# 128 bytes left free ahead of layer 0's weight tiles in a two-layer graph network

## The chip, the cores and the metric

The kernel runs on one core of one Trainium2 chip. The metric is the device time of one execution in microseconds (us); three runs of the kernel before took 1934.32, 1938.56 and 1939.16, so the median is 1938.56. A profiled execution has a span of 1935.9 us.

On-chip memory (SBUF) has 128 partitions. A tile has the same address, counted in bytes from the start of the partition, in all of them, and this document calls that number its address.

## What is computed

There are 4096 nodes with 512 features and a dense 4096x4096 adjacency matrix `adj` that is mostly zeros. The reference, cut to what matters:

```python
# layer 0
bw = sign(L0_gnn_weight); ba = max(sign(x), 0)
xw = ba @ bw.T
x = layernorm(x + relu(adj @ xw))
# layer 1
node_att = softmax(x @ node_w, axis=0)
h = x @ edge_w
e = where(adj > 0, h @ h.T, NEG_BIG)
edge_att = softmax(e, axis=1)
output = (adj * node_att * edge_att) @ (x @ weight) + bias
x = layernorm(x + output)
```

Layer 0 holds one small product (`ba @ bw.T`) and one large one (`adj @ xw`, 4096x4096 by 4096x512). Layer 1 holds the attention scores `h @ h.T` (4096x4096) and a second product of that size by 4096x512.

## The kernel before

Everything is cut into blocks of P = 128 rows: NB = 32 blocks of nodes, KD = 4 blocks of features, W = 512 columns for the moving operand of a matmul. A matmul on TensorE (PE) has two operands in SBUF: the stationary one, 128x128, which a weight load (LDWEIGHTS, "PEld" in the profile) brings into the array, and the moving one, here 512 columns wide, which streams through it. In `nc.tensor.matmul(out, a, b)`, `a` is the stationary and `b` the moving operand.

**Layer 0, first part.** `whole(g)` makes 512 rows of `xw` at a time, for g = 0 to 7. DVE turns a piece of x into 0/1 signs (`ba`, lines 186, 187, 211, 212) and the weights into signs (`bw`, lines 204 and 206); the matmuls of line 214 have `ba` as the stationary and `bw` as the moving operand; the results go to the large tile `xw` (lines 220 to 223). Two sign values are packed into one number, which is why a matmul of line 214 serves two blocks of rows. Before the first data land, line 200 runs matmuls on the tile `warm`, which holds zeros; further ones fill gaps between the first matmuls of line 214.

**Layer 0, second part.** For each block of 128 rows of `adj` (loop over `n`), the block arrives in two loads of 1 MB (`at`, line 358). Each half is handled in two quarters of 8 blocks of 128 columns. ACT casts a quarter to fp32r (`hi`, line 363), DVE subtracts to get what the cast lost (`lo`, line 365), and PE multiplies both by the same rows of `xw`:

```python
for c in range(QC):
    kb = half * HB + q * QC + c
    nc.tensor.matmul(acc, hi[:, c, :], xw[:, kb, :], start=(kb == 0), stop=False)
    nc.tensor.matmul(acc, lo[:, c, :], xw[:, kb, :], start=False, stop=(kb == NB - 1))
```

These are lines 373 and 374: 64 matmuls for each of 30 blocks, all 128x128 by 128x512 in fp32r. The other two blocks (`early`) are multiplied by `follow(g)` (lines 246 and 247) between the steps of the first part, in the same way. `hi` and `lo` have two buffers each. After a block is done, `rest` normalises it on DVE and ACT, PE transposes it (line 333), and pieces go to HBM for layer 1. Beside this, `premask` loads pieces of `adj` on the ACT queue and writes masks.

**Layer 1.** Line 101 makes `h`, lines 641 and 714 the scores, line 1081 the second large product; line 603 transposes. All of these matmuls are in fp32, and their operands are `hT`, `lops`, `right`, `slot`, `lent` and `lop`.

**What sets the order.** The tile framework orders instructions by its own costs and dependencies, except on DVE and ACT in the main loop of layer 0, where the written order holds (`manual_schedule`). Each engine works through its own list and waits for semaphores.

**Where tiles lie.** Pools are laid out one after the other in the order in which they are opened: `const`, `big`, `rows`, `small`, then for layer 0 `wide`, `stream`, `weights` (`wp`), `signs` (`sp`). Inside a pool, tiles with different tags follow each other. `big` holds one tile of 64 KB, called here the large buffer: it is `xw` in layer 0, later `hT`, then `over`. `wp` begins with `warm`, followed by `bw`, `us`, `ba` and smaller tiles; tiles with the same tag share a place (`bw`, `pair` and `we_s`; `us` and `ends`; `ba`, `single` and `sums_l`). `sp` holds the two buffers of `lo` and then those of `hi`. The pools of layer 1 (`slots`, `lopp`, `pan`) are opened after those of layer 0 are closed and take their space again from the end of `small`.

Addresses of the tiles that PE reads in layer 0, in the kernel before:

| tile | role in a matmul | address | remainder by 512 |
|---|---|---|---|
| xw | moving, lines 246, 247, 373, 374 | 17472 | 64 |
| bw | moving, line 214 | 182848 | 64 |
| ba | stationary, line 214 | 195136 and 199232 | 64 |
| lo | stationary, lines 247, 374 | 209472 and 213568 | 64 |
| hi | stationary, lines 246, 373 | 217664 and 221760 | 64 |

One row block of `xw` is 2048 bytes long, one block of `hi`, `lo` or `ba` 512.

Of the kernel before, what the change touches and what calls it, by code (L numbers as in the profile page):

```python
# [11 lines left out]
F32 = mybir.dt.float32  # L12
# [6 lines left out]
P = 128  # L19
# [10 lines left out]
def kernel(  # L30
# [13 lines left out]
    nc = tc.nc  # L44
# [114 lines left out]
    with (  # L159
# [5 lines left out]
        x1T = wide.tile([P, KD, N], F32, name="x1T")  # L165

        warm = wp.tile([P, W], BF16, name="warm")
        nc.vector.memset(warm, 0.0)
        w0 = stream.tile([P, KD, D], F32, name="w0", tag="stream")

# [1286 lines left out]
```

## Time and profile before

| what | value |
|---|---|
| median of three runs | 1938.56 us |
| span of the profiled execution | 1935.9 us |
| PE busy | 1916.8 us (99%) |
| weight loads busy | 1203.3 us (62%) |
| DVE busy | 1390.0 us (72%) |
| ACT busy | 1022.9 us (53%) |
| GpSimd (POOL) busy | 291.9 us (15%) |
| matmuls | 6742 |
| DMA traffic | 508.72 MB, mean 263 GB/s |
| first and last matmul of lines 373 and 374 start at | 57.3 us, 507.0 us |

Busy time of PE is from the start of a matmul to its modelled end, and successive matmuls overlap, so neither the busy share nor the mean duration of a matmul tells how many fit into a stretch of time. For that one reads the distance between the starts of successive matmuls, here called the spacing. A group line gives the source line, the engine, the operation, the tiles (result<-operands), the shape and the count, then the busy time in us and the mean duration in ns, then the idle time of that engine just before these instructions and what ended it.

### The profile page before, as it was taken

To read this page: it belongs to the slowest core of one execution; us is meant where nothing else is said; L and a number is where in the kernel's file an instruction comes from. 1 tells how busy PE (TensorE), PEld (TensorE's weight loads), DVE (VectorE), ACT (ScalarE), POOL (GpSimd) and SP (SyncE) were. 2 spreads that over 40 slices of the span, in tenths; PEclk is the share of its full clock that TensorE was granted. 3 is DMA by queue.
4 is the path that set the end of the run, shared out by engine and by line. 5 is a ranking of instruction groups with operands and counts; after the bars stand their busy time and mean duration, and the time that the engine had idled before them with its cause. 6 is when DMAs were issued, how large, how long until landed. Compare 5 with 4: busy or idle time off the path is not lost.

```text
span 1935.9 us, 20238 instructions
## 1 busy us (share of the span) xinstructions
PE 1916.8 (99%) x6742; PEld 1203.3 (62%) x6742; DVE 1390.0 (72%) x2062; ACT 1022.9 (53%) x1614; POOL 291.9 (15%) x413
## 2 busy tenths in 40 slices
PE   9999999999999999999999999999999999999998
PEld 6888888888644445454555444456666666666655
DVE  7766676676765567566664996687869987798737
ACT  5433333333202567576677675546766577757731
POOL 0122222222341101011111111111111110111100
PEclk9999999999999999999999999999999999999999
DMA  8888888888475478577783998777778777877731
GB/s 309 295 326 308 298 315 313 322 310 292 153 268 219 156 259 313 188 275 254 290 309 104 346 342 288 259 273 257 269 263 293 260 269 262 294 274 258 272 110 44
DMA packets 169527, 508.72 MB, mean 263 GB/s; under 512 B 15696, under 2 KB 41040, under 8 KB 161744
## 3 DMA queue, kind: packets, MB, share of 16 engines
q1 hardware_dynamic: 89472, 226.39, 35.0%
q0 software_dynamic: 64688, 239.10, 32.9%
q10 hardware_dynamic: 15264, 41.95, 5.9%
q8 instruction: 53, 0.87, 0.2%
q14 instruction: 50, 0.41, 0.1%
HBM read 385.74 MB, written 121.63 MB: 262 GB/s over the span
## 4 chain that ended last, share of the span: by engine, by line
PE 81%; DVE 9%; issue 4%; DMA 4%; ACT 1%; POOL 0%; POOLq 0%; DVEq 0%; SPq 0%
PE bank L1081 26%; PE seven L714 14%; PE acc L374 11%; PE acc L373 11%; PE pe L641 6%; PE seven L101 4%; PE po L1208 3%; PE pt L603 2%; DMA slot<-s_d 1%; DVE lent L847 1%; DMA lent<-s_d 1%; PE acc L246 1%; PE pw L214 1%; DVE lent L835 1%; PE pt L333 1%
## 5 line engine op out<-in xcount | busy, mean ns | idle before, releaser
L1081 PE MATMUL bank<-lent,lop 128*128 128x512 f32 (+1 forms) x1136 | 420.0, 517 | 0.0
L373 PE MATMUL acc<-xw,hi 128*128 128x512 f32 x960 | 376.4, 392 | 0.0
L374 PE MATMUL acc<-xw,lo 128*128 128x512 f32 x960 | 374.3, 390 | 0.0
L1081 PE MATMUL bank<-slot,lop 128*128 128x256 f32 (+1 forms) x1052 | 356.1, 486 | 1.6 <-DVE slot L862 1.6
L1081 PEld LDWEIGHTS bank<-lent,lop 128*128 128x128 f32 x1136 | 215.7, 190 | 173.9 <-issue 159.3
L1081 PEld LDWEIGHTS bank<-slot,lop 128*128 128x128 f32 x1052 | 199.6, 190 | 135.3 <-issue 115.8
L363 ACT CAST hi<-at 128x1024 fp32r<-128x1024 f32 x120 | 126.4, 1054 | 203.4 <-PE acc L373 148.4
L365 DVE TENSOR_TENSOR lo<-at,hi 128x1024 fp32r<-128x1024 f32 x120 | 147.0, 1225 | 85.2 <-ACT hi L363 85.2
L374 PEld LDWEIGHTS acc<-xw,lo 128*128 128x128 f32 x960 | 180.3, 188 | 37.1 <-DVE lo L365 0.3
L373 PEld LDWEIGHTS acc<-xw,hi 128*128 128x128 f32 x960 | 180.3, 188 | 36.7
L1090 ACT COPY over<-bank 128x512 f32<-128x512 f32 x200 | 114.4, 581 | 111.6 <-PE bank L1081 99.4
L641 PE MATMUL pe<-hT 128*128 128x512 f32 (+3 forms) x384 | 132.1, 486 | 0.0
L574 ACT ACTIVATE line<-line,nmax_c 128x512 f32<-128x512 f32 x160 | 114.8, 724 | 22.5 <-DVE nmax_c L565 22.3
L565 DVE CUSTOM_DVE_ANT_0 line<-lent,slot 128x512 f32<-128x512 bf16 x140 | 90.7, 689 | 48.4 <-ACT slot L651 26.6
L835 DVE CUSTOM_DVE_ANT_1 lent<-lent,line 128x2048 f32<-128x2048 f32 x40 | 91.4, 2286 | 20.8 <-DMA lent<-s_d 12.0
L838 ACT ACTIVATE lent<-lent 128x2048 f32<-128x2048 f32 x40 | 76.5, 1912 | 53.1 <-DVE lent L835 53.0
L841 ACT ACTIVATE slot<-slot 128x2048 f32<-128x2048 f32 x36 | 68.8, 1912 | 65.2 <-DMA slot<-in_adj_t_dram 58.3
L641 PEld LDWEIGHTS pe<-hT 128*128 128x128 f32 x384 | 64.6, 191 | 41.4 <-issue 33.8
L714 PE MATMUL seven<-hT 128*128 128x512 f32 x192 | 89.8, 593 | 0.0
L1053 ACT COPY bank<-over 128x512 f32<-128x512 f32 x144 | 84.9, 595 | 3.0 <-DVE left L973 0.2
L603 PEld LDWEIGHTS pt<-ident,lent 128*128 128x128 f32 x418 | 52.2, 141 | 52.1 <-issue 38.8
L604 ACT COPY slot<-pt 128x512 f32<-128x512 f32 (+3 forms) x123 | 68.5, 559 | 23.9 <-PE pt L603 23.9
(262 smaller groups left out, 2850.3 us busy)
## 6 DMA issues: line engine op xcount, KB each, us to landing
at<-in_adj_t_dram SPq DMA_DIRECT2D x60, 1024.0 KB, 6.8
lop<-lop_d SPq DMA_DIRECT2D x79, 512.0 KB, 4.7
lent<-s_d POOLq DMA_DIRECT2D x39, 1024.0 KB, 7.4
slot<-in_adj_t_dram POOLq DMA_DIRECT2D x38, 1024.0 KB, 7.0
s_d<-slot POOLq DMA_DIRECT2D x30, 1024.0 KB, 7.1
lent<-in_adj_t_dram POOLq DMA_DIRECT2D x26, 1024.0 KB, 7.4
lop<-lop_d SPq DMA_DIRECT2D x99, 256.0 KB, 4.2
lent<-in_adj_dram SPq DMA_DIRECT2D x48, 512.0 KB, 5.3
```

The costliest lines, as they stand in the source:

```text
L363: nc.scalar.copy(hi, aq)
L365: nc.vector.tensor_sub(lo, aq, hi.bitcast(F32))
L373: nc.tensor.matmul(acc, hi[:, c, :], xw[:, kb, :], start=(kb == 0), stop=False)
L374: nc.tensor.matmul(acc, lo[:, c, :], xw[:, kb, :], start=False, stop=(kb == NB - 1))
L565: nc.vector.tensor_tensor_reduce(line, mask, src, -1.0, HUGE, ALU.add, ALU.min, accum_out=nmax_c[:, b, c : c + 1])
L574: nc.scalar.activation(line, line, AF.Exp, bias=nmax_c[:, b, c : c + 1], scale=-1.0, accum_out=sum_c[:, b, c : c + 1])
L603: nc.tensor.transpose(pt[:, j, :], src[:, ts(j, P)], ident)
L641: nc.tensor.matmul(pe[:, lo * P :], hT[:, k, ts(A * BG + i, P)], hT[:, k, (B * BG + lo) * P : (B + 1) * W], start=(k == 0), stop=(k == KD ...
L714: nc.tensor.matmul(ps, left[m][:, k, q, :], right[m][:, k, :], start=(first and k == 0), stop=(k == KD // 2 - 1), skip_group_check=not first,)
L835: pinned[0](nc.vector._custom_dve(TENSOR_ADD_SAT, out=q, in0=q, in1=m, s0=0.0, s1=-HUGE))
L1081: nc.tensor.matmul(ps, lop[:, k, :], rop[:, k, :], start=start, stop=(k == K - 1), skip_group_check=True)
L1090: nc.scalar.copy(self.to(), self.bank[:, : self.w])
```

## The change

A tile of 32 fp32 numbers per partition, 128 bytes, is opened in the pool `wp` right behind `warm`, and set to zero once so that it is a written tile. Nothing reads it. All that follows in `wp`, and the pool `sp` behind it, has addresses higher by 128: `bw` 182976, `ba` 195264 and 199360, `lo` 209600 and 213696, `hi` 217792 and 221888. The large buffer with `xw` stays at 17472, and so do the tiles of layer 1. It is for changing where the two operands of layer 0's matmuls lie towards each other, with the same work.

```diff
         x1T = wide.tile([P, KD, N], F32, name="x1T")
 
         warm = wp.tile([P, W], BF16, name="warm")
+        room_w = wp.tile([P, 32], F32, name="room_w")
+        nc.vector.memset(room_w, 0.0)
         nc.vector.memset(warm, 0.0)
         w0 = stream.tile([P, KD, D], F32, name="w0", tag="stream")
```

Line numbers in this document are those of the kernel before; behind the added lines they are higher by two in the kernel after.

## The prediction

> **What bounds the kernel now.** The page's first two parts come first: who is busy, and at what clock.
>
> ```profile
> PE 1916.8 (99%) x6742; PEld 1203.3 (62%) x6742; DVE 1390.0 (72%) x2062; ACT 1022.9 (53%) x1614; POOL 291.9 (15%) x413
> ...
> PEclk9999999999999999999999999999999999999999
> ```
>
> PE is busy 99% of the span at full clock, so time moves only if a matmul's spacing changes or PE is made to wait. Next, the chain that ended last, by line:
>
> ```profile
> PE bank L1081 26%; PE seven L714 14%; PE acc L374 11%; PE acc L373 11%; PE pe L641 6%; PE seven L101 4%; PE po L1208 3%; PE pt L603 2%; DMA slot<-s_d 1%; DVE lent L847 1%; DMA lent<-s_d 1%; PE acc L246 1%; PE pw L214 1%; DVE lent L835 1%; PE pt L333 1%
> ```
>
> Tiles that the change moves are read by PE in L373 and L374 (22% together), L246, L247 and L214, and all of these belong to layer 0; the 26% of L1081 and 14% of L714 read other tiles, which stay. The stage by its window (columns: stretch and length; busy time of PE, weight load, DVE, ACT, POOL; clock; DMA share; GB/s):
>
> ```profile
> 48.00:512.00 464.00, 463.99 (x2094) 381.42 (x2093) 323.98 (x497) 154.72 (x193) 108.01 (x151) 1.00 0.83 301
> ```
>
> PE has no gap in 464 us, while DVE has 140 us free, ACT 309 us, and the DMA engines 17%. The groups of that stage say who waits for whom:
>
> ```profile
> L373 PE MATMUL acc<-xw,hi 128*128 128x512 f32 x960 | 376.4, 392 | 0.0
> L374 PE MATMUL acc<-xw,lo 128*128 128x512 f32 x960 | 374.3, 390 | 0.0
> ...
> L363 ACT CAST hi<-at 128x1024 fp32r<-128x1024 f32 x120 | 126.4, 1054 | 203.4 <-PE acc L373 148.4
> L365 DVE TENSOR_TENSOR lo<-at,hi 128x1024 fp32r<-128x1024 f32 x120 | 147.0, 1225 | 85.2 <-ACT hi L363 85.2
> ```
>
> ACT waits 148 us for PE to free a hi buffer; PE waits for neither. The 392 ns are one matmul from start to modelled end and overlap with the next, so the price is the spacing of starts, read from the timeline (start, duration, engine):
>
> ```profile
> 300.09 0.39 PE L374 MATMUL acc<-xw,lo 128*128 128x512 f32 x1
> 300.09 0.19 PEld L373 LDWEIGHTS acc<-xw,hi 128*128 128x128 f32 x1
> 300.32 0.39 PE L373 MATMUL acc<-xw,hi 128*128 128x512 f32 x1
> 300.32 0.19 PEld L374 LDWEIGHTS acc<-xw,lo 128*128 128x128 f32 x1
> ...
> 301.45 0.39 PE L374 MATMUL acc<-xw,lo 128*128 128x512 f32 x1
> ```
>
> From 300.09 to 301.45 are six steps: 0.227 us each. Each weight load starts with the matmul before it and takes 0.19 us, inside 0.227, so the length of the load is not what spaces the matmuls. Other matmuls of this trace are spaced closer for the same 512 columns:
>
> ```profile
> 1124.72 4.03 PE L1081 MATMUL bank<-lent,lop 128*128 128x512 f32 x9
> ```
>
> ```profile
> 10.00 1.04 PE L200 MATMUL idle<-warm 128*128 128x512 bf16 x4
> ```
>
> Nine fp32 matmuls take (4.03 - 0.59)/8 = 0.430 us each, twice 0.215; four bf16 ones (1.04 - 0.39)/3 = 0.217. So an fp32r matmul of layer 0 pays 11 to 12 ns beyond the 0.215 that the same width takes elsewhere. That is the only quantity in the trace that an address could plausibly own, and the whole question.
>
> [...] the 0.227 stays the same whether ACT and DVE work beside it or not, but something takes 11 ns. [...]
>
> **The change, part by part.**
>
> *What moves.* In the built program's allocation, room_w takes 128 bytes per partition right after warm, and bw, us, ba, nw_b, bias_b, scr, hi and lo (and the tiles sharing their places: pair, single, ends, we_s, t1 to t4) go up by 128. xw, at, x1T, rows, lop, slot and lent stay, so layer 1 from L641 on keeps every address. Before, xw (17472), hi (217664), lo (209472), bw and ba all leave 64 when divided by 512, and the steps inside them are multiples of 512. Afterwards the four moved ones leave 192 and xw still 64. So only the pair xw against hi or lo changes its distance (L373, L374, L246, L247); in L214 both operands move together.
>
> *The memset.* One DVE instruction of 128x32 ahead of warm's. The trace has 0.06 us for 128x1 and 0.27 for warm's; about 0.08 us. DVE then waits until 4.86 us for w0 to land, and the warm-up matmuls, which start 0.08 later, end at 5.78 + 0.08, ahead of the first real one at 6.48. Hidden: 0.
>
> *Order.* POOL and ACT keep their orders. On PE, one warm-up matmul passes from ahead of the third pair of L214 to behind it. The pair waits for DVE's ba anyway; the group behind grows from four to five, ending its starts at 10.00 + 5 x 0.217 = 11.08, where the fourth pair now starts at 10.90. Cost 0 to 0.2 us. On SP one 1 MB load of at comes ahead of two 256 KB loads of xb; ACT's wait for PE (148 us) says that at is early. 0.
>
> *DVE, ACT, DMA on shifted tiles.* Free time of 140 and 309 us in the stage covers several per cent of their work. Destination addresses of DMAs keep their remainder by 128. Taken as 0.
>
> *Spacing of fp32r matmuls.* The trace has no run with other distances, so this is bounded. There are 960 + 960 + 64 + 64 = 2048 that change distance; about 1960 of them run without a gap. Low end: [...] 11 ns each, -22 us. High end: the slowest spacing in the trace when matmul and load are out of step, just after a transpose (starts at 313.02 and 313.25, with neighbours, average 0.23 and reach 0.236): +9 ns, +18 us. I take 0, for this reason: all 1920 products of L373 and L374 step through 32 rows of xw, 8 blocks of hi or lo and two buffers each, and their distance takes every multiple of 512 in turn, yet the spacing stays at 226 to 227 ns. L214, with quite other tiles, has the same 227. A cost that depends on addresses could only repeat within 512 bytes, which is possible but is a narrow door; a cost that belongs to fp32r matmuls as such explains all of it. Sum: 0.1 us, that is 1938.5.
>
> **Rivals.**
> - *The distance was the cost* (faster). For it: every pair of operands now stands at a distance that is a multiple of 512, the spacing is 11 ns above both other types, and it wanders between 228 and 236 after a transpose until matmul and load are in step again, so the two streams do touch. Against: fp32 matmuls of layer 1 have the same remainders and pay nothing. 1938.5 - 22 = 1916[...].
> - *The new distance is worse* (slower). For it: the same wandering, which shows that 236 can happen. Against: it must hold for most blocks. 1938.5 + 18 = 1957.
> - *A moved DVE or ACT operand gets slow* (slower). If L365 took twice its 147 us, DVE would need 324 + 147 = 471 us of 464 and PE would wait: +7 us, 1946. Nothing in the trace speaks for it; counted with the one before.
>
> **How the numbers follow.** No change: 0.49. Faster through the distance: 0.31; the excess of 11 ns is there to be won, and the two streams do touch, so a dependence within 512 bytes can't be excluded. Slower, either way: 0.20. The likeliest is no change, 1938.5. The range takes in the no-change case to +6 us (0.3%, and repeats of before spread over 1934 to 1939) and the faster one to its 1911-1916, and leaves out the slower: 1912 to 1945.
>
> **What would show it.** Right: starts of L373 and L374 stay 0.227 apart, the window of the stage stays 464 us long. If the distance matters, L373, L374, L246 and L247 change their spacing and L214 keeps 0.227; if L214 changes with them, the place itself counts and not the distance. If DVE or ACT got slow, L365 or L363 has another mean than 1225 or 1054 ns and PE shows idle time ended by them. A change of layer 1's spacing would be outside of everything here. The prediction fails if two reads of PE meet within 512 bytes.

## The result

The changed kernel takes 1949.64 us (median of four runs, 1944.63 to 1950.38), the kernel before 1938.03 (four runs, 1934.32 to 1939.16): ratio 1.0058, 95% interval 1.0036 to 1.0080. It is slower by 11.6 us, above the stated range (1912 to 1945) and on the side that had been given 2 chances in 10.

The first part of the profile after shows PE as full as before and busy 11 us longer, on the same 6742 matmuls; the busy times of the others moved by less than 2 us.

```profile
PE 1927.7 (99%) x6742; PEld 1204.3 (62%) x6742; DVE 1390.9 (72%) x2063; ACT 1022.5 (53%) x1614; POOL 293.4 (15%) x413
```

The groups of layer 0 after (line numbers are higher by two: L375 and L376 are L373 and L374 of before; L365 and L367 are L363 and L365):

```profile
L375 PE MATMUL acc<-xw,hi 128*128 128x512 f32 x960 | 383.7, 400 | 0.0
L376 PE MATMUL acc<-xw,lo 128*128 128x512 f32 x960 | 376.9, 393 | 0.0
...
L365 ACT CAST hi<-at 128x1024 fp32r<-128x1024 f32 x120 | 125.9, 1049 | 211.5 <-PE acc L375 159.4
L367 DVE TENSOR_TENSOR lo<-at,hi 128x1024 fp32r<-128x1024 f32 x120 | 147.0, 1225 | 92.6 <-ACT hi L365 92.5
```

The two matmul groups went from 392 and 390 ns to 400 and 393; PE still waits for nothing ahead of them. ACT and DVE take the same time for one instruction as before, within 0.5% (1054 and 1225 ns then), and ACT waits 11 us longer for PE. So no wait was added: the matmuls themselves follow each other more slowly. Their starts in the timeline after, in the middle of the stage:

```profile
300.12 0.40 PE L375 MATMUL acc<-xw,hi 128*128 128x512 f32 x1
300.36 0.39 PE L376 MATMUL acc<-xw,lo 128*128 128x512 f32 x1
300.59 0.40 PE L375 MATMUL acc<-xw,hi 128*128 128x512 f32 x1
300.83 0.39 PE L376 MATMUL acc<-xw,lo 128*128 128x512 f32 x1
...
301.99 0.40 PE L375 MATMUL acc<-xw,hi 128*128 128x512 f32 x1
```

From 300.12 to 301.99 are eight steps (a step is the spacing from one start to the next), 0.234 us each, where they were 0.227. Read in ns, the steps alternate: 237 to 238 after a product with hi, 229 after one with lo, in 24 of 30 blocks, 233.3 on average. Five of the other six blocks settle at 232.2 to 232.5; the second block holds two groups of transposes and changes its pattern, the sequence in which the steps repeat, at each of them. In the 24 blocks the steps are the same whether ACT and DVE are at work beside them or both idle (237.5 ns after hi and 229.2 after lo each time), so it is not their reading and writing of the shifted tiles that slows PE.

The clock is not what changed: the clock row of the profile after has a 9 in all 40 slices, as before, and the granted clock of the stage is 1.00 both times. The stretch from the first of these matmuls to the last as a window, before and after (the clock is the third number from the end):

```profile
57.00:508.00 451.00, 450.99 (x2048) 373.04 (x2047) 313.38 (x482) 147.54 (x182) 108.01 (x151) 1.00 0.84 303
```

```profile
57.00:519.00 462.00, 462.00 (x2049) 373.33 (x2048) 313.68 (x482) 147.16 (x182) 108.01 (x151) 1.00 0.82 295
```

The starts of L373 and L374 together run from 57.33 to 507.02 us before, those of their counterparts from 57.34 to 517.83 after: 449.7 against 460.5, so this stage alone loses 10.8 us. The two profiled spans differ by 6.7 only (1935.9 and 1942.6), because the rest of the profiled execution after is 4 us shorter: 2 us in the stage of L101 (96.4 against 98.4), 2 us from the first score matmul to the end (1327.2 against 1329.4). The changed layer 0 is not the reason. L101 takes 96.4 us also in three of the kernels below whose layer 0 is as fast as before (everything moved; only weights and signs moved; layer 1 moved), and the kernel below in which hi and lo alone are moved loses 11.0 us in this stage and has a span 11.4 us longer than before (1947.3 us). The profiled run of after is also the fastest of its four; the other three are at 1949 to 1950. Where the last 2 us come from is not known.

### The profile page after: what moved, and what is told of

It is laid out like the page before. It is cut to its first block, busy times and chain, and to the rows that moved or that the text cites. A ratio compares the mean times of both kernels' runs of the same rounds, so it can differ in the third digit from the quotient of the medians.

```text
span 1942.6 us, 20239 instructions
## 1 busy us (share of the span) xinstructions
PE 1927.7 (99%) x6742; PEld 1204.3 (62%) x6742; DVE 1390.9 (72%) x2063; ACT 1022.5 (53%) x1614; POOL 293.4 (15%) x413
## 4 chain that ended last, share of the span: by engine, by line
PE 83%; DVE 8%; issue 4%; DMA 3%; ACT 1%; POOL 0%; DVEq 0%; POOLq 0%
PE bank L1083 25%; PE seven L716 15%; PE acc L375 12%; PE acc L376 11%; PE pe L643 6%; PE seven L101 5%; PE po L1210 3%; PE pt L605 3%; DVE lent L849 1%; DMA slot<-s_d 1%; PE acc L248 1%; DMA lent<-s_d 1%; DVE lent L837 1%; PE pt L335 1%; PE pw L216 1%
## 5 line engine op out<-in xcount | busy, mean ns | idle before, releaser
L375 PE MATMUL acc<-xw,hi 128*128 128x512 f32 x960 | 383.7, 400 | 0.0
L376 PE MATMUL acc<-xw,lo 128*128 128x512 f32 x960 | 376.9, 393 | 0.0
L365 ACT CAST hi<-at 128x1024 fp32r<-128x1024 f32 x120 | 125.9, 1049 | 211.5 <-PE acc L375 159.4
L367 DVE TENSOR_TENSOR lo<-at,hi 128x1024 fp32r<-128x1024 f32 x120 | 147.0, 1225 | 92.6 <-ACT hi L365 92.5
L375 PEld LDWEIGHTS acc<-xw,hi 128*128 128x128 f32 x960 | 180.4, 188 | 44.5
L376 PEld LDWEIGHTS acc<-xw,lo 128*128 128x128 f32 x960 | 180.4, 188 | 39.6
L840 ACT ACTIVATE lent<-lent 128x2048 f32<-128x2048 f32 x40 | 76.5, 1912 | 58.8 <-DVE lent L837 58.6
L843 ACT ACTIVATE slot<-slot 128x2048 f32<-128x2048 f32 x36 | 68.8, 1912 | 63.8 <-DMA slot<-in_adj_t_dram 53.5
```

Source lines behind the costliest of these rows:

```text
L365: nc.scalar.copy(hi, aq)
L367: nc.vector.tensor_sub(lo, aq, hi.bitcast(F32))
```

## The experiments

The theory after the result: what counts is the **distance** in bytes between the moving operand (xw) and the stationary ones (hi, lo), and it repeats after some power of two. Rivals: the **place** of a tile by itself (its remainder by 512); the **memset and the changed order** at the start; the **weights and signs** (bw, ba), which moved as well.

### All distances in two kernels

hi and lo get 512 bytes more in each buffer and lie at another offset in them with every block of rows. The diff shows hi; lo is treated in the same way. The second kernel has 31 - n in place of n - 2, so that its distances fall where those of the first rise. The work is the same.

```diff
-hi = sp.tile([P, QC, P], F32R, name="hi", tag="hi")
+hi = sp.tile([P, QC * P + P], F32R, name="hi", tag="hi")
+hi = hi[:, 4 * (n - 2) : 4 * (n - 2) + QC * P].rearrange("p (c w) -> p c w", w=P)
 nc.scalar.copy(hi, aq)
...
```

> hi and lo lie 16 bytes further from xw with every block of rows: block k (0 to 29) at distance 16k beyond a multiple of 512; bw and ba stay. Theory distance: the spacing of L373 and L374 follows the distance. Block 0 gives 226.7 ns, block 8 (128 bytes) 233.3, and the other distances give other values between 213 and 245, the same whether distances rise or fall from block to block. Theory place of the tile (remainder by 512 of hi and lo alone): same curve, told apart by the run in which all tiles move. Rival, drift or order of the stage: all blocks near one value, no curve.

> The same offsets in the reverse order: block k at distance 464 - 16k. Theory distance: the curve of spacing against distance is that of the rising sweep within 1 ns, so block 29 gives 226.7 and block 21 233.3. Rival, order of the stage: the curve follows the number of the block, not the distance.

Two blocks of the rising kernel in its timeline, the first at a distance of 240 bytes (block 15), the second at 288 (block 18):

```profile
295.06 0.39 PE L375 MATMUL acc<-xw,hi 128*128 128x512 f32 x1
295.29 0.39 PE L376 MATMUL acc<-xw,lo 128*128 128x512 f32 x1
...
296.20 0.39 PE L376 MATMUL acc<-xw,lo 128*128 128x512 f32 x1
```

```profile
339.64 0.40 PE L375 MATMUL acc<-xw,hi 128*128 128x512 f32 x1
339.88 0.40 PE L376 MATMUL acc<-xw,lo 128*128 128x512 f32 x1
...
341.04 0.40 PE L375 MATMUL acc<-xw,hi 128*128 128x512 f32 x1
```

Five steps in 1.14 us, 0.228 each; six steps in 1.40 us, 0.233 each: the same program, one position of the same two tiles against another. Mean spacing in ns over the later three quarters of each block (from the 17th matmul on, without the steps at a transpose):

| distance mod 256 | rising, first 256 | rising, second 256 | falling, first 256 | falling, second 256 |
|---|---|---|---|---|
| 0 | 226.7 | 226.7 | 226.7 | 226.7 |
| 16 | 231.6 | 233.3 | 233.3 | 233.4 |
| 32 | 233.3 | 233.4 | 233.3 | 233.3 |
| 48 | 233.3 | 233.3 | 233.3 | 233.3 |
| 64 | 233.4 | 233.4 | 233.3 | 233.4 |
| 80 | 232.0 | 232.0 | 232.0 | 232.0 |
| 96 | 234.2 | 234.2 | 234.3 | 234.3 |
| 112 | 233.3 | 233.3 | 233.3 | 233.3 |
| 128 | 233.3 | 233.3 | 232.4 | 232.4 |
| 144 | 233.3 | 233.3 | 233.3 | 233.3 |
| 160 | 233.3 | 233.3 | 233.4 | 233.3 |
| 176 | 230.1 | 230.1 | 229.9 | 229.9 |
| 192 | 228.8 | 228.8 | 229.0 | 229.4 |
| 208 | 231.8 | 231.7 | 231.9 | 231.9 |
| 224 | 233.3 | | 233.4 | |
| 240 | 226.7 | | 226.7 | |

The curve follows the distance and not the number of the block: the four columns agree to within 0.9 ns, but for 16 in the first column, and it repeats after 256 bytes. The kernel before stands at its lowest value. No distance came near 213, the lower end of what was expected. One execution of each kernel took 1945.86 and 1947.92 us.

Two distances show two steady patterns. At 128 the rising kernel has 233.3 and the falling one 232.4, and the trace after shows both. At 16 the odd value of the first column, 231.6, is a mean of two patterns in one block, block 1 of the rising kernel, which changes over at a group of transposes:

```profile
81.23 0.40 PE L375 MATMUL acc<-xw,hi 128*128 128x512 f32 x1
...
82.63 0.40 PE L375 MATMUL acc<-xw,hi 128*128 128x512 f32 x1
...
84.26 0.60 PE L333 MATMUL pt<-ident,xb 128*128 128x128 f32 x4
...
85.16 0.39 PE L376 MATMUL acc<-xw,lo 128*128 128x512 f32 x1
...
86.52 0.39 PE L376 MATMUL acc<-xw,lo 128*128 128x512 f32 x1
```

Six steps take 1.40 us ahead of the transposes, 0.233 each, and 1.36 behind them, 0.227 each, at the same distance (modulo 256). So at some distances it also counts how matmuls and loads have fallen into step.

In these two kernels the place of hi and lo changes together with their distance from xw. The two are parted further down, for 128 bytes alone.

### Which of the two tiles, and products of half the width

Six kinds of block in turn: hi and lo get offsets of their own, and in the last two kinds each product is cut in two.

```diff
+kind = (n - 2) % 6
+hi_at, lo_at = (0, 32, 0, 32, 0, 32)[kind], (0, 0, 32, 32, 0, 32)[kind]
+pieces_ = [(0, 256), (256, 256)] if kind > 3 else [(0, 512)]
...
```

> Six kinds of block in turn: nothing moved; hi alone by 128; lo alone by 128; both by 128; then nothing moved and both moved with each product cut into two of 256 columns, which loads the same weights twice. Theory, a weight load meets the matmul running beside it: with hi alone moved the spacing after L374 (beside which hi is loaded) rises to about 233 to 238 and the one after L373 stays at 227; with lo alone the other way round. Rival, the matmul pays for its own operands: the spacing after L373 rises with hi moved. [...]

| kind | after hi | after lo | mean |
|---|---|---|---|
| nothing moved | 226.7 | 226.7 | 226.7 |
| hi alone by 128 | 230.9 | 233.6 | 232.2 |
| lo alone by 128 | 233.6 | 230.9 | 232.2 |
| both by 128 | 237.4 | 229.2 | 233.3 |
| nothing moved, cut | 120.0 | 120.0 | 120.0 |
| both by 128, cut | 118.7 | 118.6 | 118.7 |

The values are spacings in ns, those of most of the five blocks of a kind. In the first block with hi alone moved and the first with lo alone, a second pattern appears behind a group of transposes: steps of 232 to 235, 233.3 on average. With one tile moved the larger loss is at the matmul beside which that tile is loaded, as the theory of the neighbouring load has it; but the other one does not stay at 227, so the two are coupled, and this run alone does not decide. The cut products, nothing moved, in the timeline:

```profile
124.83 0.28 PE L380 MATMUL acc<-xw,hi 128*128 128x256 f32 x1
124.95 0.28 PE L381 MATMUL acc<-xw,lo 128*128 128x256 f32 x1
...
125.43 0.28 PE L381 MATMUL acc<-xw,lo 128*128 128x256 f32 x1
125.55 0.28 PE L380 MATMUL acc<-xw,hi 128*128 128x256 f32 x1
```

Each takes 0.120 us for 256 columns, where half of the 226.7 ns for 512 would be 113.3. An estimate from these two spacings: (226.7 - 120.0) / 256 = 0.417 ns for each column, and 13.3 ns that do not grow with the columns. So at distance 0 the excess is about 13.3 ns for each matmul with its weight load, not a share of its columns. Whether the load or the fp32r matmul as such costs them is not shown, since every fp32r matmul here has a load of its own. And at 128 the cut products are not slower but faster by 1.3 ns (118.7 against 120.0). So 128 bytes is not bad as such; which distance is good differs here between 256 and 512 columns.

### Distance, place or memset

128 bytes and a memset in the first pool: everything that matters moves together, and the remainder by 512 becomes 192 for all.

```diff
     node_s = const.tile([P, NB], F32, name="node_s")
+    room_c = const.tile([P, 32], F32, name="room_c")
+    nc.vector.memset(room_c, 0.0)
```

> 128 bytes and their memset stand in the first pool, so that xw, bw, ba, hi, lo and all tiles of layer 1 move by 128 together; distances are those of the kernel before, remainders by 512 are 192 as in the changed kernel. Theory distance: spacing 226.7 ns, time that of before, ratio 0.998 to 1.002. Theory place: spacing near 233 ns, ratio near 1.006. Rival, memset and order of the first instructions: ratio near 1.006 with spacing at 226.7.

Ratio 0.9999, interval 0.9992 to 1.0007 (1937.48 us). Its two groups:

```profile
L375 PE MATMUL acc<-xw,hi 128*128 128x512 f32 x960 | 376.5, 392 | 0.0
L376 PE MATMUL acc<-xw,lo 128*128 128x512 f32 x960 | 374.1, 390 | 0.0
```

They are those of before. The place of the tiles by itself and a memset at the start cost nothing that can be measured. What is left is the distance of hi and lo from a tile that stayed where it was in the changed kernel. In L373 and L374 PE reads only xw beside them, and whether ACT and DVE were at work made no difference to the steps; where the moving operand itself starts elsewhere, further down, bears this out.

### The period, and one part of the change alone

First, the changed kernel with twice the room:

```diff
-        room_w = wp.tile([P, 32], F32, name="room_w")
+        room_w = wp.tile([P, 64], F32, name="room_w")
```

> The changed kernel with 256 bytes of room in place of 128: bw, ba, hi and lo have moved, the memset is there, the distance of hi and lo from xw is a multiple of 256. Theory, the distance counts with a period of 256 bytes: spacing 226.7 ns, ratio to before 0.998 to 1.002. Rival, any departure from a multiple of 512 costs, or the move as such: spacing near 233 ns and ratio near 1.006.

Ratio 0.9997, interval 0.9989 to 1.0005 (1937.56 us). Moving the same tiles by 256 bytes, with the same memset in the same place, costs nothing that can be measured.

Second, the changed kernel with 384 bytes more ahead of lo and hi, which makes 512 for these two, so that only bw, us and ba keep the shift by 128:

```diff
         x1T = wide.tile([P, KD, N], F32, name="x1T")
+        room_s = sp.tile([P, 96], F32, name="room_s", tag="room", bufs=1)
+        nc.vector.memset(room_s, 0.0)
```

> bw, us and ba have moved by 128 bytes as in the changed kernel, hi and lo by 512, which restores their distance modulo 512. Theory distance of hi and lo: ratio to before 0.998 to 1.002. Rival, the moved weights and signs carry part of the loss: ratio 1.002 to 1.004.

Ratio 0.9998, interval 0.9990 to 1.0006 (1937.46 us).

Third, the kernel before with 128 bytes ahead of lo and hi alone (the same two lines with 32 in place of 96, and no room_w):

> Only the pool of hi and lo moves by 128 bytes, bw, us and ba stay. Theory distance of hi and lo: the whole loss of the changed kernel, spacing 233.3 ns or, in the other steady pattern, 232.4, ratio to before 1.004 to 1.008. Rival, weights and signs carry it: ratio below 1.002.

Ratio 1.0061, interval 1.0048 to 1.0074 (1949.91 us), and the groups are like those of the changed kernel:

```profile
L375 PE MATMUL acc<-xw,hi 128*128 128x512 f32 x960 | 384.2, 400 | 0.0
L376 PE MATMUL acc<-xw,lo 128*128 128x512 f32 x960 | 376.7, 392 | 0.0
```

The whole loss sits with hi and lo.

### Steps of 4 bytes around zero

> hi and lo of block k (0 to 29) at distance 4k - 60 bytes from a multiple of 256. From the coarse sweep: 226.7 ns from -16 to 0, 233 at +16, 232 at -48. Theory, lines of 16 bytes: the spacing steps at multiples of 16 and is level between them. Rival, a finer grain: it changes with every 4 bytes, and some distance near 0 may lie below 226.7, which would give a kernel faster than both.

The kernel is the rising one with an offset of 49 + n - 2 elements of 4 bytes in place of 4 * (n - 2), which is -60 to +56 bytes from a multiple of 256. Spacing in ns:

| distance | -60 | -56 | -52 | -48 | -44 | -40 | -36 | -32 | -28 | -24 | -20 | -16 | -12 | -8 | -4 |
|---|---|---|---|---|---|---|---|---|---|---|---|---|---|---|---|
| spacing | 233.4 | 231.0 | 234.9 | 231.9 | 236.7 | 232.3 | 233.3 | 233.3 | 231.2 | 231.1 | 231.6 | 226.6 | 233.3 | 233.3 | 233.3 |

| distance | 0 | 4 | 8 | 12 | 16 | 20 | 24 | 28 | 32 | 36 | 40 | 44 | 48 | 52 | 56 |
|---|---|---|---|---|---|---|---|---|---|---|---|---|---|---|---|
| spacing | 226.7 | 232.3 | 230.6 | 230.0 | 226.7 | 233.3 | 231.2 | 233.3 | 233.3 | 233.3 | 233.4 | 230.0 | 233.3 | 233.3 | 233.3 |

Level steps of 16 bytes are not what this shows: -12, -8 and -4 lie high between two low points, and 0, 4, 8 and 12 all differ. The other expectation falls too: nothing is below 226.6. But each distance occurs in one block only. At +16 this kernel shows 226.7, the low one of the two patterns that the rising sweep had there, while the sweeps had mostly 233.3; so some of the other values may also be one pattern of two. With full 512 columns, the multiples of 256 and the points 16 bytes below them (-16 here, 240 in the sweeps) were low, at 226.6 to 226.7 ns, each time they were run. No version faster than the kernel before follows from this.

### Own weights or those of the neighbour

To part the two, the moving operand of one of the products starts 32 columns later, so that the distance to a matmul's own weights and the distance to those loaded beside it can be set independently. Those 32 columns are left out of the sum.

```diff
+kind = (n - 2) % 5
+hi_at, lo_at = (0, 32, 32, 32, 0)[kind], (0, 0, 0, 32, 0)[kind]
+hi_w = slice(0, W - 32) if kind in (0, 3) else slice(32, W) if kind == 1 else slice(0, W)
+lo_w = slice(32, W) if kind == 2 else slice(0, W)
...
```

> Five kinds of block in turn; in some the product with hi or with lo leaves out 32 columns, so that its moving operand starts 128 bytes later or ends earlier (those columns of the sum are left out). Kind 0: nothing moved, hi on the first 480 columns. Kind 1: hi moved by 128 and its moving operand too, lo plain; each matmul lies at distance 0 from its own weights, and at 128 from the weights loaded beside it. Kind 2: hi moved, lo's moving operand moved; distance 128 from its own weights and 0 from those loaded beside it. Kind 3: hi and lo moved, hi on the first 480 columns; 128 both ways. Kind 4: plain. Theory, a matmul meets the weight load that runs beside it: a pair of matmuls takes 440 ns in kinds 0 and 2 (213.3 + 226.7), about 453 in kinds 1 and 3, and 453.3 in kind 4, which has the full width. Rival, it meets its own weights: 440 in kinds 0 and 1, about 453 in kinds 2 and 3.

| kind | distance to own weights | to those loaded beside it | a pair takes, ns |
|---|---|---|---|
| 0 | 0 | 0 | 446.7 |
| 1 | 0 | 128 | 448.9 |
| 2 | 128 | 0 | 446.7 |
| 3 | 128 | 128 | 450.0 |
| 4 (plain, full width) | 0 | 0 | 453.3 |

A block of kind 1 and one of kind 2 in the timeline; 20 pairs lie between the two lines of each:

```profile
150.91 0.38 PE L380 MATMUL acc<-xw,hi 128*128 128x480 f32 x1
...
159.89 0.38 PE L380 MATMUL acc<-xw,hi 128*128 128x480 f32 x1
```

```profile
165.72 0.39 PE L380 MATMUL acc<-xw,hi 128*128 128x512 f32 x1
...
174.65 0.40 PE L380 MATMUL acc<-xw,hi 128*128 128x512 f32 x1
```

They take 8.98 and 8.93 us. In both kinds hi and lo lie at the same places and one product of each pair is 32 columns short; what differs is which product that is, and with it where the moving operand starts. This fits the distance from xw, and not a distance between hi or lo and a tile that PE does not read here. Kinds 0 and 2 agree to 0.1 ns, 1 and 3 are slower than kind 0 by 2.2 and 3.3. So it is mainly the weights loaded beside a matmul that matter, and the rival, for which kind 2 had to be like kind 3, falls; the 1.1 ns between kinds 1 and 3 are not explained. The size failed: 13 ns were expected between the two groups, and kind 0 itself takes 446.7 where 440.0 had been expected. That was an estimate: 226.7 for the full width, and 213.3 for 480 columns, which is 226.7 less 32 columns of 0.417 ns. With unequal lengths the even step of 226.7 ns is lost even at distance 0 (after hi 215 ns, after lo 232).

### The same shift in layer 1, in fp32

```diff
     lopp = ctx.enter_context(tc.tile_pool(name="lopp", bufs=4))
+    room_l = lopp.tile([P, 32], F32, name="room_l", tag="room", bufs=1)
+    nc.vector.memset(room_l, 0.0)
```

> Only lop, the stationary operand of L1081 in fp32, moves by 128 bytes (and the small tiles behind it); layer 0 is as before. Theory, the distance matters [...] in fp32r alone: the spacing of L1081 stays at 429 to 430 ns for 512 columns and 216 for 256, ratio 0.998 to 1.002. Rival, it matters for fp32 too: each of the 2188 matmuls loses up to 6.7 ns, the spacing rises to 436 and 222, and the ratio to about 1.007.

```profile
L1083 PE MATMUL bank<-lent,lop 128*128 128x512 f32 x736 | 324.8, 592 | 0.0
L1083 PE MATMUL bank<-slot,lop 128*128 128x512 f32 x528 | 232.1, 592 | 1.3 <-DVE slot L864 1.3
```

Busy time and mean are those of L1081 before (324.8 and 592, 232.1 and 592); the median spacing stays at 429 ns for 512 columns and 216 for 256. Ratio 0.9994, interval 0.9985 to 1.0002 (1936.46 us). The fp32 matmuls of L1081 do not feel these 128 bytes. No other distance was tried for them, and why they are spared is not shown.

## Why the prediction was wrong

- **The bound, the stage and the quantity were right.** PE is full in layer 0, and the spacing of fp32r matmuls is what moved. The step that failed is the last of the parts: "I take 0". It should have been +6.7 ns on most of the 1920 products of L373 and L374. At 233.3 against 226.7 ns throughout that would be 1920 x 6.7 = 12.8 us; the trace has 10.8, mainly since the first ten or so matmuls behind the transposes of a block were unsettled and slow before the change too (about 230 ns on average) and lose little more.
- **The reason given for 0 was too weak for what it carried.** All distances in the kernel before were multiples of 512, and equal spacing among them could only show that nothing happens between multiples of 512. The prediction said so itself ("a narrow door") and gave the door small odds; the effect repeats after 256 bytes and varies inside them, so the door was the whole of the question. The load of the next weights is not without effect on the running matmul here: where the neighbouring weights lie changes a pair from 446.7 to 448.9 ns (kinds 0 and 1 of the crossed distances).
- **The first rival had the wrong sign.** It took the 10 to 12 ns above the 215 to 217 of the other types as the price of the distance. But 512 columns took 226.7 ns at distance 0, and no distance that was tried took less than 226.6. The lowest time given for this rival, 1911 us, was the author's estimate and rests on no spacing in the trace. The kernel before was already at the lowest spacing found, and with 512 columns every shift that was tried cost something or did nothing. That part of the prediction's reason, a cost of fp32r matmuls that no address takes away, fits the runs with 512 columns.
- **The second rival was right in kind and too large.** It took +9 ns from the unsettled matmuls after a transpose, 18 us; measured were 6.7 ns on the steady ones, 10.8 us in the stage and 11.6 in the whole. The unsettled steps gave the right direction and not the size of a settled pattern. They were the one place of the trace of before where this spacing was seen to be worse, and it deserved more weight than 2 in 10.
- **The argument from fp32** (same remainders, no cost) did not carry over: the fp32 matmuls pay nothing at 128 either (429 ns at both distances), so they say nothing on fp32r.
- **The rest held.** Memset and order cost nothing (ratio 0.9997 with the same memset and 256 bytes; the first product of L373 starts at 57.34 us against 57.33); ACT and DVE kept their durations; layer 1 kept its spacing (a median of 429 ns for 512 columns in L101, L641, L714 and L1081, before and after). L246 and L247, which also read xw, went from a median of 227 to 232 ns (mean 231.0 to 232.1, since many were unsettled before). L214, whose operands moved together, still settles at 226 to 227 in five of its seven groups of eight, as before, though it now takes longer to settle: before, four of the seven kept that spacing from their first step on, after, none.
- **The third rival**, a slow ACT or DVE operand, did not occur: 1225 ns before and after for L365, 1054 and 1049 for L363.

What stays open is the mechanism. Shown: moving hi and lo by 128 bytes against xw makes the whole loss; the spacing repeats after 256 bytes of distance; it is mainly the distance to the weights loaded beside a matmul that counts; fp32 shows nothing at 128; and the cost depends on the pattern into which matmuls and loads fall (two patterns at 128 and at +16; the opposite sign with cut products). Not shown: that at other distances than 128 the place of hi and lo plays no part. What it is that repeats after 256 bytes is not shown either. A fixed cost of each load at 128 bytes does not fit: the cut products are faster there (118.7 ns against 120.0).

## What to carry to other kernels

When one engine is full for hundreds of microseconds, compare the spacing of its instructions with that of other types in the same trace. Treat any tile shift (a new small constant, another pool order) as a change to be measured where fp32r matmuls with a fresh weight load each are involved: here 128 bytes made 6.7 ns of 227, and 11.6 us of 1938. Placing moving and stationary operands at a distance that is a multiple of 256 bytes kept the low spacing, 226.7 ns, in every run with full 512 columns in both products; with 256 columns 128 bytes was better (118.7 against 120.0), so for another width the distance has to be measured anew. Offsets that change from block to block test thirty distances in one run, but a value seen once may be one of two patterns. And an argument from constancy covers only the values that really occurred.

## What was not expected of the hardware

- The spacing of fp32r matmuls with a weight load each does not halve with the width: at distance 0 it is 226.7 ns for 512 columns and 120.0 for 256, by estimate 13.3 ns beside the columns, although for 512 columns the load beside it takes only 0.19 of the 0.227 us.
- The distance between the moving operand and the weights changes the spacing for 512 columns by up to 10 ns (236.7 at -44 bytes against 226.7 at 0), with a period of 256 bytes.
- Two steady patterns can exist at one distance (233.3 and 232.4 at 128; 226.7 and 233.3 at 16), and a group of transposes can switch between them.
- Products of 256 columns are faster at 128 bytes (118.7) than at 0 (120.0).
